# Four layers of cross attention and mixture of experts: routing the tokens per batch, the first batch inside the attention stream

## The chip, the cores and the metric

The kernel runs on one core of a Trainium2 chip. The metric is the device time of one execution in microseconds (us); before the change the median of three runs is 2267.55 (2266.69 to 2267.87). The engines are named as in the profile: PE (matrix multiply) and PEld (its weight loads), DVE (vector), ACT (scalar, with the function tables), POOL (GpSimd) and SP, whose queue issues most of the plain DMAs. Indirect DMAs (scatters and gathers by row number) are issued by POOL. All data is float32.

## What is computed

The state `x` has 2 batches of 512 tokens of width 256; the context has 2 batches of 1024 rows of width 256. Four layers follow each other, each a cross attention and a mixture of experts, both added to the state:

```python
x = x + L0_xattn(layernorm(x), ctx);  x = x + L0_ffn(layernorm(x))
x = x + L1_xattn(ctx, layernorm(x));  x = x + L1_ffn(layernorm(x))
x = x + L2_xattn(layernorm(x), ctx);  x = x + L2_ffn(layernorm(x))
x = x + L3_xattn(layernorm(x), ctx);  x = x + L3_ffn(layernorm(x))
```

- Attention: L0 has 16 heads of 64 with scores clipped to ±11; L1 8 heads of 64, whose keys are the context and the state itself; L2 16 heads of 16, causal; L3 16 heads of 16 with rotary positions.
- Mixture of experts, 8 experts each. A router gives every token 8 logits. L0: softmax, the best expert, its result times the probability (gated SiLU, inner width 1024). L1: the best expert on rows scaled by the sigmoid of the logit (inner width 512), plus a shared expert for all tokens. L2: the two best, weights by a softmax over their two logits (ReLU, 1024). L3: first `h = rmsnorm(x @ W_in.T)`; the router and the experts work on `h`; the two best (gated SiLU, 1024), each result RMS-normed, the weighted sum RMS-normed again and multiplied by `W_out`.

## The kernel before

The state stays in SBUF as `X`, 8 tiles of 128 tokens by 256; tiles 0 to 3 are batch 0 and 4 to 7 batch 1. The program is written with a framework whose scheduler places instructions on the engines by program order as priority and by its own model of when they are ready.

**Attention streams.** Work is cut into groups (a batch and some heads; batch 0 comes first) and slots of a group: L0 16 groups of 4 slots, L1 8 of 6, L2 8 of 8, L3 8 of 16. A slot issues scores of one group and products of an earlier one. What belongs to a whole group (query projection `pq`, division, output projection `po` at L1391, the addition to `X` at L1394) is put into a queue of Python generators, `Pieces` (L203), and the slots call a piece now and then between their own work; `share` (L218) spreads what is left over the places that are left, `drain` (L225) runs the rest, and `run_stream` (L230) drives L0 and L1. PE's order in a stream is fixed as written (`pe_in_order`, L188). L2 and L3 share `attend16` (L1202): a first pass (scores at L1298, their maxima on DVE at L1308), `with_maxima` (L1313), a second pass (scores L1355, exponentials on ACT L1356, and in L2 the causal mask on POOL, `affine_select` at L1360), products (L1331), and `divide` (L1365). When a batch's last group is divided, `add_out` (L1387) is queued as four pieces. Scores and pieces take their PSUM banks from one set of seven.

**Routing, after the attention of each layer, for all 8 tiles at once.** The layer norm of `X` (L72 to L98), transposes (L117) and their copies to SBUF, both on ACT (L122); the router logits, two matmuls in two passes per tile, that is 32 instructions (`router_logits`, L251); the choice of the best or the two best, small DVE operations on 128 x 64 (`first_of`, `two_best`, `two_gates`, L269 to L301); and `slots_of` (L332). That one counts, by 9 matmuls of triangular and all-ones matrices (L347 and L349, 18 instructions), how many tokens in front go to the same expert, and from it gives each token a slot: each expert owns one tile of 128 slots, and what doesn't fit goes to overflow tiles behind them. It also finds each overflow tile's expert (`wrow`) and the number of overflow tiles (`used`, read into registers).

`moe` (L404) then scatters the rows to their slots in DRAM (`xd`, L424): one indirect DMA for each tile and pick, so 8 in L0 and L1, 16 in L2 and L3. With two picks a token number rides in each row (column 257); DVE rewrites it for the second pick (L423), after the first pick's scatter of that tile has read the row. Behind them stands the filler, PE work that waits for no scatter: in L0 and L2 the next layer's keys and values (`ahead1`, `ahead16`, L545 to L617), in L1 the shared expert (L1467), in L3 none. Then the slot tiles run: weights of one expert (`w`, SP at L438, or POOL by row number for overflow tiles, L445), rows (`xs`, L452, which wait for all scatters), two transposes, the expert's matmuls (first `pa`, then `pg`, `y`), and the results to DRAM. `combine` (L530) or `add_results` (L519) gather them and add them to `X` with the gates.

L3's part (L1521 to L1589) has more steps before the router: norm and transposes, `ph` (`xT` times `W_in`), an ACT copy for each tile to `h` (L1556), the RMS norm of `h` (squares on ACT L1537, scaling on DVE L1546), transposes to `hnT`. Each FFN loads its router's weights (`rw`, in L0 with the bias `rb`, in L3 with `w_in`, `eb`, `inw`) when its pools are opened.

Of the kernel before, what the change touches and what calls it, by code (L numbers as in the profile page):

```python
# [17 lines left out]
P = 128  # L18
# [15 lines left out]
def tile_kernel(ctx: ExitStack, tc: tile.TileContext, d: dict, out: bass.AP):  # L34
# [50 lines left out]
    def norm_to(dst, src, norm, ts=None, split=False):  # L85


        t0, mv, r = norm
        if split:
            nb = small.tile([P, mv.shape[1]], F32, tag=f"nb{mv.shape[1]}", name="nb")  # L90
            nc.vector.scalar_tensor_tensor(nb, mv[:, :, 0], -1.0, r, ALU.mult, ALU.mult)
        for t in range(mv.shape[1]) if ts is None else ts:
            if split and t % 2:
                nc.scalar.activation(
                    dst[:, t0 + t, :], src[:, t0 + t, :], AF.Identity, bias=nb[:, t : t + 1], scale=r[:, t : t + 1]
                )
                continue
            nc.vector.tensor_scalar(  # L98
                dst[:, t0 + t, :], src[:, t0 + t, :], mv[:, t, 0:1], r[:, t : t + 1], ALU.subtract, ALU.mult
# [103 lines left out]
    class Pieces:  # L203
# [14 lines left out]
        def share(self, places):  # L218

            self.due += max(self.left, 0) / places  # L220
# [9 lines left out]
    def run_stream(n_groups, slots, lag, unit, prep, steps):  # L230
# [4 lines left out]
        while t < n_groups * slots + lag or pieces.queue:  # L235
# [4 lines left out]
            if u == slots - 1:  # L240
# [4 lines left out]
    def bc8(a):  # L245
        return a[:, :, None].to_broadcast([P, TT, E])

    def rt(name, shape=(TT, E)):
        return small.tile([P, *shape], F32, tag=f"rt_{name}", name=name, bufs=1)

    def router_logits(ps, srcT, w):  # L251
        pl = ps.tile([P, TT, E], F32, tag="mm", name="pl")
        for t in range(TT):
            mm2(pl[:, t, :], srcT, slice(t * P, (t + 1) * P), w, slice(0, E))
        lg = rt("lg")
        nc.vector.tensor_copy(lg, pl)
        return lg

    def maxed(src, name):
        m = rt(name, (TT,))  # L260
        nc.vector.tensor_reduce(m, src, AX.X, ALU.max)
        return m

    def summed(src, name):
        m = rt(name, (TT,))
        nc.vector.tensor_reduce(m, src, AX.X, ALU.add)
        return m

    def first_of(src, m, name):  # L269

        oh = rt(name)
        nc.vector.tensor_tensor(oh, src, bc8(m), ALU.is_equal)
        nc.vector.tensor_mul(oh, oh, rank)
        k = maxed(oh, "first_k")
        nc.vector.tensor_tensor(oh, oh, bc8(k), ALU.is_equal)
        return oh

    def two_best(src):
        oh1 = first_of(src, maxed(src, "m1"), "oh1")
        rest = rt("rest")  # L280
        nc.vector.scalar_tensor_tensor(rest, oh1, -3.0e38, src, ALU.mult, ALU.add)
        oh2 = first_of(rest, maxed(rest, "m2"), "oh2")
        return oh1, oh2

    def two_gates(lg, oh1, oh2):

        t = rt("pick")
        s = rt("sel", (2, TT))
        for i, oh in enumerate((oh1, oh2)):
            nc.vector.tensor_mul(t, oh, lg)  # L290
            nc.vector.tensor_reduce(s[:, i, :], t, AX.X, ALU.add)
        m = rt("selm", (TT,))
# [10 lines left out]

    def expert(ps, hp, srcT, w1, w2, F, act, glu, consume):

        FT = F // P
        for tb in range(2):
            cols = slice(tb * 512, (tb + 1) * 512)
            hT = hp.tile([P, FT, 512], F32, tag="hT", name="hT")
            for f in range(FT):  # L310
                pa = ps.tile([P, 512], F32, tag="a", name="pa")
                mm2(pa, w1, slice(f * P, (f + 1) * P), srcT, cols)
# [4 lines left out]
                mm2(pg, w1, slice(F + f * P, F + (f + 1) * P), srcT, cols)  # L317
# [14 lines left out]
    def slots_of(ps, picks, n_over):  # L332
# [3 lines left out]


        oh = rt("oh_all", (2 * TT + 1, E))
        nc.vector.memset(oh, 0.0)
        own = oh[:, TT : 2 * TT, :]  # L340
        if len(picks) == 1:
            nc.vector.tensor_copy(own, picks[0])
        else:
            nc.vector.tensor_add(own, picks[0], picks[1])

        pr = ps.tile([P, TT + 1, E], F32, tag="mm", name="pr")
        nc.tensor.matmul(pr, below, oh[:, TT:, :], start=True, stop=False)  # L347
        for k in range(1, TT + 1):
            nc.tensor.matmul(pr, ones, oh[:, TT - k : 2 * TT + 1 - k, :], start=False, stop=(k == TT))  # L349
        r = rt("rank_in", (TT + 1, E))  # L350
        nc.vector.tensor_copy(r, pr)
# [1407 lines left out]
```

## Time and profile before

| | us |
|---|---|
| median of three runs | 2267.55 (2266.69 to 2267.87) |
| the profiled execution | 2271.06 |
| its span | 2269.0 |
| L0 attention, FFN | 0 to 468.8, to 690.0 |
| L1 attention, FFN | to 1079.3, to 1235.0 |
| L2 attention, FFN | to 1400.7, to 1626.0 |
| L3 attention, FFN | to 1935.2, to 2269.0 |
| busy over the span: PE, DVE, ACT, POOL | 2087.4 (92%), 1085.2 (48%), 866.2 (38%), 438.6 (19%) |

The borders are the ends of the additions to `X` that close an attention, and the starts of the next one's first work; neighbouring stages overlap a little. The windows view gives the busy time of every engine in such a stretch, with the clock that was granted to PE (1.00 is full). The chain of waits goes back from the last instruction, at each step to what released it. Both speak of one execution, the profiled one.

### The profile page before, as it was taken

The page shows a single profiled execution, that of the slowest core. Times are in us where ns is not written, and L with a number is a line of the kernel's source. Part 1 is how long each engine was busy: PE and PEld are TensorE (multiplying, and loading weights), DVE is VectorE, ACT ScalarE, POOL GpSimd, SP SyncE. Part 2 cuts the span into 40 slices and gives each one's busy share as a digit, 9 for nine tenths or more (in the row PEclk, how much of TensorE's full clock was granted, in tenths as well). Part 3 has the DMA queues.
Part 4 walks back from the last instruction along what each step waited for, and adds up shares of the span by engine and source line. Part 5 has one row for each costly group of instructions (what it writes and reads, how often), then busy time and mean ns, then how long its engine had stood idle before and what let it go on. Part 6 is the DMA issues. An engine that isn't in the chain of part 4 may idle for free. (4 is left out here: it accounts for less than half of the span.)

```text
span 2269.0 us, 30730 instructions
## 1 busy us (share of the span) xinstructions
PE 2087.4 (92%) x11892; PEld 1267.6 (56%) x11892; DVE 1085.2 (48%) x2161; ACT 866.2 (38%) x1657; POOL 438.6 (19%) x420
## 2 busy tenths in 40 slices
PE   7999999999998999999898898899599999579996
PEld 3444444358984444555586344599333333479995
DVE  7766666741115656655313884110387773322223
ACT  4444444421115655555112333222135556223333
POOL 2222223210012111111101122312123310111110
PEclk9999999999999999999899999999789999689998
DMA  4222221277744101001454512687311101657771
GB/s 128 70 61 75 75 72 50 83 269 283 302 162 136 38 28 38 28 10 51 156 211 153 213 35 90 219 320 293 101 47 30 34 15 25 250 187 288 315 306 63
DMA packets 112328, 301.21 MB, mean 133 GB/s; under 512 B 23344, under 2 KB 76849, under 8 KB 103473
## 3 DMA queue, kind: packets, MB, share of 16 engines
q1 hardware_dynamic: 76624, 159.79, 21.0%
q0 software_dynamic: 9888, 104.49, 12.0%
q10 hardware_dynamic: 25664, 34.90, 4.3%
q8 instruction: 98, 1.61, 0.3%
q14 instruction: 54, 0.43, 0.1%
HBM read 243.42 MB, written 47.66 MB: 128 GB/s over the span
## 5 line engine op out<-in xcount | busy, mean ns | idle before, releaser
L1356 ACT ACTIVATE p<-s 128x512 f32<-128x512 f32 (+3 forms) x384 | 186.3, 546 | 176.2 <-PE s L1355 115.4
L132 PE MATMUL pa<-sT,w 128*128 128x128 f32 x1920 | 236.0, 277 | 10.7 <-DVE sT L462 3.7
L132 PEld LDWEIGHTS pa<-sT,w 128*128 128x128 f32 x1920 | 227.3, 193 | 19.3 <-ACT sq L1537 5.7
L480 PE MATMUL y<-w,hT 128*128 128x256 f32 x960 | 221.8, 383 | 12.4 <-DVE hT L477 6.3
L1298 PE MATMUL s<-kT,qT 32*128 32x512 f32 (+3 forms) x768 | 218.2, 613 | 10.0 <-DVE nm L1304 4.9
L480 PEld LDWEIGHTS y<-w,hT 128*128 128x128 f32 x960 | 178.5, 191 | 37.7 <-DVE hT L477 8.5
L1355 PE MATMUL s<-qA,kT 32*128 32x512 f32 (+3 forms) x768 | 196.1, 586 | 1.3 <-ACT p L1356 0.9
L1308 DVE TENSOR_REDUCE mx<-s 128x1 f32<-128x512 f32 x256 | 163.5, 686 | 56.1 <-PE s L1298 35.4
L477 DVE TENSOR_TENSOR hT<-act,pg 128x512 f32<-128x512 f32 x82 | 56.0, 688 | 233.5 <-PE pg L132 204.6
L1043 ACT ACTIVATE p<-s,nm 128x512 f32<-128x512 f32 x192 | 129.6, 687 | 84.0 <-DVE nm L1040 84.0
L132 PE MATMUL pg<-sT,w 128*128 128x128 f32 x1312 | 160.0, 275 | 1.3 <-ACT sv L575 1.3
L878 ACT ACTIVATE p<-s 128x1024 f32<-128x1024 f32 x128 | 124.3, 1023 | 89.7 <-PE s L873 89.7
L879 DVE TENSOR_SCALAR p<-p 128x1024 f32<-128x1024 f32 x128 | 108.9, 859 | 95.2 <-ACT p L878 95.2
L132 PEld LDWEIGHTS pg<-sT,w 128*128 128x128 f32 x1312 | 153.1, 192 | 1.4 <-ACT sv L575 1.4
L1040 DVE TENSOR_REDUCE nm<-s 128x2 f32<-128x1024 f32 x96 | 113.3, 1221 | 83.5 <-PE s L1036 83.5
L149 POOL TENSOR_TENSOR kT<-kT,turned 128x512 f32<-128x512 f32 x62 | 100.8, 1631 | 215.2 <-DVE turned L147 208.4
L884 DVE TENSOR_TENSOR acc<-acc,p 128x1024 f32<-128x1024 f32 x96 | 131.6, 1371 | 2.8
L804 PE MATMUL o<-p,v 128*64 128x512 f32 x512 | 125.7, 609 | 3.6 <-DVE p L879 3.6
L873 PE MATMUL s<-qT,kT 64*128 64x512 f32 x512 | 127.2, 615 | 0.0
L1298 PEld LDWEIGHTS s<-kT,qT 32*128 32x128 f32 x768 | 77.1, 191 | 66.7 <-issue 28.0
L1057 PEld LDWEIGHTS pt<-ident,p 128*128 128x128 f32 x768 | 86.3, 141 | 49.2 <-issue 24.5
L1331 PE MATMUL o<-p,v 128*32 128x256 f32 (+3 forms) x1280 | 106.2, 403 | 6.7 <-POOL p L1360 6.4
(282 smaller groups left out, 2955.3 us busy)
## 6 DMA issues: line engine op xcount, KB each, us to landing
w<-in_L_experts_dram SPq DMA_DIRECT2D x8, 3200.0 KB
w<-in_L_experts_dram SPq DMA_DIRECT2D x8, 3072.0 KB
w<-in_L_experts_dram SPq DMA_DIRECT2D x8, 2048.0 KB
w<-in_L_experts_dram SPq DMA_DIRECT2D x8, 1536.0 KB
kd<-sk ACTq DMA_DIRECT2D x40, 256.0 KB
kT<-kd SPq DMA_DIRECT2D x16, 512.0 KB
turned<-kT SPq DMA_DIRECT2D x60, 128.0 KB
v<-vd SPq DMA_DIRECT2D x12, 512.0 KB
```

The source lines that it names most:

```text
L132: nc.tensor.matmul(ps_ap, lhsT[:, dc, lcols], rhs[:, dc, rcols], start=(dc == 0), stop=(dc == 1))
L480: nc.tensor.matmul(y, hT[:, f, :], w2[:, f, :], start=(f == 0), stop=(f == FT - 1))
L804: nc.tensor.matmul(G[n]["o"][64 * j : 64 * j + 64, :], V[g, b][:, kt, pr * P + 64 * j : pr * P + 64 * j + 64], p[:, j, :], start=(kt == 0) ...
L873: nc.tensor.matmul(s1[:, j, :], G[n]["kT"][r, kt * P : (kt + 1) * P], G[n]["qT"][r, :], start=True, stop=True)
L878: G[n]["exp"] = nc.scalar.activation(p, s1, AF.Exp, scale=0.125).ins
L884: nc.vector.tensor_add(G[n]["acc"], G[n]["acc"], p)
L1040: nc.vector.tensor_reduce(nm[:, qt, :, c], s1, AX.X, ALU.max, negate=True)
L1043: nc.scalar.activation(p[:, j, :], s1[:, j, :], AF.Exp, bias=nm[:, qt, j, c : c + 1], accum_out=l[:, qt, j, c : c + 1],)
L1298: nc.tensor.matmul(s1[:, :w], qT[r, qt * P : (qt + 1) * P], kT[r, c * 512 : c * 512 + w], start=True, stop=True)
L1308: nc.vector.tensor_reduce(mx[:, qt, j, c : c + 1], s1, AX.X, ALU.max)
L1355: nc.tensor.matmul(s2[:, qs], kT[r, kt * P : (kt + 1) * P], qA[r, qs], start=True, stop=True)
L1356: nc.scalar.activation(p[:, j, qs], s2[:, qs], AF.Exp, scale=0.25)
```

## The change

The functions that routed all tiles at once are replaced by a class `Dispatch`, made once per layer. Its generators do the steps for one batch of four tiles (`norm`, `turned`, `logits`, `to_slots`, the scatters included), and `last` does what needs both batches (`wrow`, `used`). `dispatch0` to `dispatch3` string them together for a layer. Batch 0 is queued as pieces into the attention's stream, when the first batch's part of `X` is final; batch 1 runs after the attention as before. `yield` marks the end of a piece; `gap` puts empty pieces between steps.

What changes with it:

- For batch 1, `to_slots` adds the counts of batch 0, and gives a second step (`far`) to ranks beyond the overflow tiles that batch 0 opened. The number of expert tiles that run is the same; the order of the overflow tiles can differ.
- The prefix matmuls are 5 per batch (10 instructions) in place of 9 for all.
- Of the two copies of a transposed batch one is on ACT, one on DVE (`copy_alt`).
- The router's weights are loaded before or at the start of the attention, into a pool that stays until the end of the layer (`apart`).
- L1's sigmoid becomes exp, +1 and a reciprocal.
- L3's `ph` is two banks of two tiles with one copy each; the first batch's scratch tiles in L3 come from four buffers of the pool `L3y`, which also take the gathered results of L2.
- At the end of a stream `run_stream` no longer drains; it goes on with slots until the queue is empty, and there `share` calls pieces as long as the queue holds any.

The core of the diff:

```diff
         def share(self, places):
 
-            self.due += max(self.left, 0) / places
+            self.due += max(self.left, places == 1 and len(self.queue)) / places
...
             unit(t, pieces)
-            if u == slots - 1:
+            if u == slots - 1 and n + 1 < n_groups:
                 pieces.drain()
...
+        def norm(self, b, pool, bank, tags=("xn", "xT")):
+
+            S = self.S[b]
+            S["rows"] = pool.tile([P, 4, self.width], F32, tag=tags[0], name="xn")
+            norm_to(S["rows"][:, :, 0:D], X, norm_of(X, 4 * b, 4), d0=0)
+            yield
+            yield from self.wait(b)
+            S["xT"] = pool.tile([P, 2, 512], F32, tag=tags[1], name="xT")
+            yield from self.turned(S["xT"], S["rows"], bank)
...
+        def to_slots(self, b, picks, bank):
...
+            pr = bank("pr")[:, 0 : 5 * E].rearrange("p (t e) -> p t e", e=E)
+            nc.tensor.matmul(pr, below, oh[:, 4:9, :], start=True, stop=False)
+            for k in range(1, 5):
+                nc.tensor.matmul(pr, ones, oh[:, 4 - k : 9 - k, :], start=False, stop=(k == 4))
...
+            yield
+            more = rt(b, "more", (E, 7))
...
+            rows, named = S["rows"], self.width > D
+            for i, si in enumerate(S["slots"]):
+                if named and i == 0:
+                    nc.vector.tensor_copy(rows[:, :, D], c_tok[:, 4 * b : 4 * b + 4])
+                for t in range(4):
+                    if i == 1:
+                        c = 4 * b + t
+                        nc.vector.tensor_scalar(rows[:, t, D:], c_tok[:, c : c + 1], float(NT), None, ALU.add)
+
+                    x = nc.gpsimd.indirect_dma_start(
+                        out=xds[self.L][0], out_offset=bass.IndirectOffsetOnAxis(ap=si[:, t : t + 1], axis=0),
+                        in_=rows[:, t, :], in_offset=None,
+                    ).ins
...
+            if t == 4 * (len(groups) - 1):
+                pieces.add(dispatch0(0, dp, banks(ps)), 10)
...
+            if (n, w) == (5, 0):
+                pieces.add(dispatch1(0, dp, lambda name: ps.tile([P, 512], F32, tag="mm", name=name, bufs=3)), 12)
...
                         if groups[m - 1][1] == 3:
                             pieces.add(add_out(groups[m - 1][0]), 4)
+                            pieces.add(dispatch(bank), 9 + 6 * rotary)
...
+        all_of(dispatch2(1, fp, banks(ps)))
+        disp.last()
...
+    def dispatch3(b, pool, bank, tags, hpool):
+
+        S = disp.S[b]
+        yield from disp.norm(b, pool, bank, tags[:2])
+        h = S["rows"] = hpool.tile([P, 4, D + 1], F32, tag="h", name="h")
+        for k in range(2):
+            ph = bank("ph").rearrange("p (t f) -> p t f", t=2)
+            for i in range(2):
+                c = (2 * k + i) * P
+                mm2(ph[:, i, :], S["xT"], slice(c, c + P), w_in, slice(0, D))
+            nc.scalar.copy(h[:, 2 * k : 2 * k + 2, 0:D], ph)
+            yield
+        rms(pool, tags[2], h, inw, 0, 4)
+        yield
+        yield from disp.wait(b)
+        hT = pool.tile([P, 2, 512], F32, tag=tags[3], name="hT")
+        yield from disp.turned(hT, h, bank)
+        yield from disp.logits(b, hT, rw, bank)
...
+        yield from disp.to_slots(b, picks, bank)
+
+    attend16(
+        "L3", params, 8, False, True, False, lambda bank: dispatch3(0, ay, bank, ["yg"] * 4, dp), first, late
+    )
```

## The prediction

> **What bounds the kernel now.** I read the windows by stage first (layer by layer, attention and FFN apart), then the chain of waits in the stages that the change touches, then the timeline at the borders. The profiled execution took 2271.06 us (span 2269.0, 2.1 around it), 3.5 over the median of three, 2267.55. I work in its clock and take the difference off the median. Columns of the windows: stretch, length, PE, PEld, DVE, ACT, POOL busy, granted clock, DMA share, GB/s. Here are L3's attention, L3's FFN and eight microseconds of the end of L0's attention.
>
> ```profile
> 452.00:456.00 4.00, 1.78 (x8) 0.20 (x4) 3.96 (x4) 0.00 (x0) 0.47 (x1) 1.00 0.00 0
> 456.00:460.00 4.00, 3.93 (x10) 1.00 (x10) 1.49 (x3) 0.00 (x0) 0.00 (x0) 0.57 0.00 0
> ...
> 1626.00:1935.20 309.20, 301.11 (x2210) 111.15 (x2210) 207.68 (x380) 151.75 (x277) 65.71 (x51) 0.95 0.12 35
> 1935.20:2269.00 333.80, 271.77 (x1884) 252.22 (x1884) 87.93 (x305) 113.00 (x207) 48.46 (x50) 0.89 0.61 239
> ```
>
> L3's attention has PE busy 97% and DVE 67%: work added to it is paid for. Its FFN has PE busy 81%, and the chain shows where the rest is: no filler covers the way from the last addition to X (ends 1935.22) to the first expert matmul (pa, 1999.19).
>
> ```profile
> 1937.08 2.19 PE pt L117 x8
> ...
> 1955.29 7.01 PE pl L132 x32
> ...
> 1966.86 3.43 PE pr L349 x16
> ...
> 1973.98 1.01 POOL xd L424
> ...
> 1993.04 2.56 DMA xd<-h,si
> ...
> 1995.79 2.08 DMA xs<-xd
> ...
> 1999.19 3.55 PE pa L132 x16
> ```
>
> That gap is 64.0 us; 19.1 of it, 1973.98 to 1993.04, is POOL issuing 16 scatters, the logits run at half speed (.219 us each; L0's 32 took 3.63 at clock 1.00, .114 each). In L0, L1 and L2 a filler (next layer's keys, or the shared expert) keeps PE busy meanwhile, so only L3's gap is bare.
>
> **L3, the gap.** Each per-token step halves. Scatters 16 to 8, at a pitch of 19.06/15 = 1.27: −10.2. Logits 32 to 16: −3.5. Copies and squares on ACT (1942.27 to 1949.24, .87 a tile), four tiles less: −3.5. Transposes of xn (4.06): −2.0. Scaling and transposing h (2.87 + 1.77): −2.3. Prefix matmuls 18 to 10 (4.1): −1.8. Choice (narrower rows): −.3. Six more slot operations in the chain at .22: +1.3. Sum −22.3, taken as −22; the new gap is 42. The 14 small operations of `last` (14 × .2 = 3) lie behind eight scatters (10.1); uncovered they cost 3. The first weights, issued 1934.83 and in flight until 1965.3, put a floor of some 30 under it: not reached.
>
> **L3, the stream.** PE takes on 16 transposes (1.04 per 8: 2.1), 16 ph matmuls (3.62), 16 logits (1.8), 10 prefix (1.25): 8.7. What does PE work cost there? The chain holds one pq a group:
>
> ```profile
> 1796.72 1.91 PE pq L132 x4
> ...
> 1813.68 1.92 PE po L1391 x8
> ...
> 1835.82 1.91 PE pq L132 x4
> ```
>
> Groups lie 31.65 apart (1733.43 to 1765.08, to 1796.72) without po, and 39.10 with four po of 1.92: 7.45 longer for 7.68 of work, .97 for one. So +8.5. ACT gets the square roots among the exponentials: two pairs of table loads at 1.28, 5.1 on an engine that is half free; I take +1.5 of 0 to 5. DVE gets some 13 us (about 45 small operations at .2, four applies at .33, four scalings at .41, copies at .6) into its free third of two groups (23). And a wait comes with it: between the picks DVE rewrites the token number (L423) of each tile, which waits for that tile's first scatter. Before, these stood 1.2 apart after a first 2.3, so four hold DVE for about 6, and behind it queue the maxima (mx, 1.3 a slot) that free PSUM banks for PE's next scores. Seven banks and the scheduler, which may put maxima between, hide most: +1 of 0 to 6. Stream +11 (5 to 18); L3 −11 (−17 to −4).
>
> One page of the Trainium skill speaks against this. The row first: at 2078.75 a table load takes 1.28 and the square root follows at 2080.05, so 1.30 a switch. "ScalarE: Activation LUTs", section "What ACT_TABLE_LOAD costs", adds a drain of about 1.38 to the load's 1.28, 2.66 a switch; by it L3's four would be an estimated 10.6 instead of 5.1, and with the same share falling on PE's path (1.5 of 5.1) the stream would cost 3.1 for them and the whole sum come to −7. No drain is seen in that row, so the row decides.
>
> **L1.** Its filler starts late because the router weights are late and PE's clock is cold:
>
> ```profile
> 1088.87 6.97 PE L132 MATMUL pl<-rw,xT 128*128 128x8 f32 x32 [4.62 <-DMA rw<-in_L_ffn_router_wT_dram]
> 1095.69 2.06 PE L132 MATMUL pa<-xT,w 128*128 128x512 f32 x2
> ```
>
> With the weights loaded before the attention, 4.62 of waiting and half of the logits (3.5) go, and half of the prefix (1.8), which ran inside the filler. What is late next is the shared expert's w1, issued 1083.7 to 1084.6 and by rw's 5.6 us an estimated 1090 to 1091.6 on the chip; so −7 (−5 to −9). The filler ended 1143.6 and the experts began 1144.99, so it passes on. The stream gets 8 transposes, 16 logits, 10 prefix: 4.1 on a PE that is 96% busy, and 1 for tables: +5. L1 −2 (−6 to +1).
>
> **L0.** The dispatch falls into the last slots, about 436 to 460, where DVE sets the pace (3.96 of 4 busy in the first line above, PE 1.78; the clock of .57 in the second is PE coming back from that idleness). A unit there is 3.79 us: PE 1.99 for scores and 1.94 for products, DVE twice .69 and 1.23, 3.84. The dispatch adds some 8 us of DVE work (applies, one copy, some 30 small operations; the statistics of batch 0 already ran there before); of the 22 us from 436 to 458 DVE had 3.3 free: +5, and 1 for the tables. Behind, PE's filler ended 508.2 and the rows landed about 507, together; PE loses 3.8 of work (8 transposes 1.04, 16 logits 1.8, 8 prefix 1.0), the scatters shift by more: −4. L0 +2 (−4 to +7).
>
> **L2.** The queue that matters is POOL's. In the causal stream POOL masks every probability tile, and PE waits for it:
>
> ```profile
> 1380.18 1.06 PE L1331 MATMUL o<-p,v 128*32 128x512 f32 x8 [1.65 <-POOL p L1360]
> 1380.54 0.41 POOL L1360 TENSOR_SCALAR_AFFINE_SELECT p<-p 128x256 f32<-128x256 f32 x1 [0.42 <-ACT p L1356]
> ```
>
> The dispatch is queued behind the first batch's four products (the last po at 1360.45) as nine pieces and more, one in each slot or every second one, of some 1.9 us. By that count the eight scatters (8 × 1.27 = 10.1 of POOL) come out near 1375 to 1385, among the last group's nine masks (1376.6 to 1387.8). Price 0 to 10.1; PE's wait of 5.3 in 1376 to 1400 is the nearest row, I take 6, a little above it, since scatters that start between two masks delay only the next. DVE's hold at the token numbers falls into the same time and is not counted twice. PE work of 4.1 costs .53 of itself (pitch 15.25, then 18.33 with three po, 5.76), +2. Behind: PE loses 4.1 before the filler's end and some 2 of stalls: −6. L2 +2 (−6 to +9).
>
> The early loads of router weights on SP's queue are small and go ahead of loads with 40 us and more to spare (L0's issue 459.75, needed 505); uncovered, the rw row's 4.6 is the price of one. No other SP instruction moves; the expert tiles are as many as before.
>
> **Sum:** −11 −2 +2 +2 = −9: 2271.06 becomes 2262, and off the median 2258.5.
>
> **Rivals.** *The streams hide it.* L3's stream pays only half (+5), as in L2 where .53 was paid; masks and scatters interleave. −17 −4 −1 +0 = −22: 2245.5. Against it stands L3's .97. *It cancels.* L3's stream pays its upper part, +16 (tables 3, the DVE hold 4.5), L1 0, L0 and L2 +3 each: −6 +0 +3 +3 = 0: 2267.5. *The scatters block the in-order queues,* on the slower side: in both two-pick streams eight scatters in one piece, 10.1, stand ahead of what the attention waits for, L2's masks and L3's rotations and maxima, at full price. L3 −22 +10 +10 = −2, L2 +2 +10 −6 = +6, L0 with DVE full +5, L1 −2: +7, 2274.5. It decides once the attention's own instruction is queued behind the first scatter rather than between two. For it speaks that DVE's L147 in L2 ran only at 1433.75, straight behind eight such waits; against it, POOL works only 21% of L3's attention. *The gap doesn't shrink,* because weights and not rows end it: excluded by the 30 us floor, short of a slower transfer.
>
> **Chances.** Forecast .42 (2251 to 2265), hidden .20, cancels .16, blocked .22. Below 2263.0 (0.2% is 4.5 us, about what can be told from no change) lie the hidden case and .36 of the forecast: .56. Within: .16 and .06: .22. Slower: .22. The range, 2243 to 2277, reaches into both outer cases and leaves out .07 below and .10 above; the forecast's own is 2251 to 2265.
>
> **What would show it.** L3: last addition to X until first pa near 42, the group with the dispatch some 11 longer. L2: masks behind scatters, attention's end later by about 8. L1: no wait for rw, filler 4 to 6 earlier after the attention. L0: attention's end later by about 6. Table loads for square roots inside all streams. The forecast falls if L3's gap stays over 50 or its stream grows by under 6 or over 16.

## The result, and the profile after

The changed kernel takes 2300.77 us (median of four runs, 2299.67 to 2311.03), the kernel before 2267.71 on the same chip (2266.69 to 2270.84): a ratio of 1.0154 [1.0123, 1.0184], 1.5% slower, where 2258.5 was forecast. The profiled execution after took 2300.8; its span is 2299.1, before 2269.0, so 30.1 longer. By the ends of the additions to `X` (for L3's FFN by the start of the last one):

| stage | before | after | difference | forecast |
|---|---|---|---|---|
| L0 attention, FFN | 468.8, 214.4 | 477.6, 213.6 | +8.8, −0.8 | +6, −4 |
| L1 attention, FFN | 396.0, 152.6 | 406.0, 144.2 | +10.0, −8.4 | +5, −7 |
| L2 attention, FFN | 168.9, 226.0 | 189.8, 234.9 | +20.9, +8.9 | +8, −6 |
| L3 attention, FFN | 308.5, 329.8 | 318.1, 310.6 | +9.6, −19.2 | +11, −22 |

L3, where the gain was expected, came out as forecast (−9.6 against −11). L2 lost 29.8 where 2 was forecast, and L0 and L1 lost 9.6 where 0 was. Here are the windows of after, with the columns of the prediction: the end of L0's stream, then L3's attention and FFN.

```profile
452.00:456.00 4.00, 4.00 (x28) 2.22 (x24) 3.88 (x5) 1.59 (x2) 1.70 (x1) 1.00 0.17 59
456.00:460.00 4.00, 4.00 (x18) 1.30 (x18) 3.86 (x9) 2.16 (x3) 0.00 (x0) 1.00 0.00 0
460.00:464.00 4.00, 0.48 (x4) 0.48 (x3) 3.29 (x11) 0.00 (x0) 0.00 (x0) 0.78 0.00 0
464.00:468.00 4.00, 4.00 (x15) 2.50 (x17) 1.99 (x15) 0.00 (x0) 0.00 (x0) 0.50 0.01 4
...
1666.10:1984.20 318.10, 308.12 (x2268) 116.93 (x2268) 218.53 (x440) 161.00 (x296) 73.47 (x59) 0.97 0.18 58
1984.20:2299.00 314.80, 261.50 (x1828) 242.65 (x1828) 85.66 (x304) 106.02 (x187) 40.69 (x42) 0.91 0.59 228
```

In L0 the stream now runs some 9 us longer; at 460 PE stands still (0.48 of 4) while DVE makes the choice, and the next four microseconds run at half clock. In L3's attention PE works 7.0 more (301.11 before) and DVE 11. That this stage met its forecast is in part luck: its time at half clock fell from 31 us to 18 (the table below), at its start, ahead of the dispatch. The chain of waits over L3's gap:

```profile
1998.52 3.60 PE pl L133 x16
...
2006.19 6.24 issue
2012.43 0.27 POOL xd L424
...
2021.32 2.43 DMA xd<-h,si
...
2023.95 1.96 DMA xs<-xd
...
2027.33 3.75 PE pa L133 x16
```

16 logits and 8 scatters instead of 32 and 16: from the last addition (1984.18) to the first `pa` it is 43.2 us, 64.0 before. In L1 nothing waits for the router weights any more; the timeline of PE:

```profile
1102.63 3.16 PE L133 MATMUL pl<-rw,xT 128*128 128x8 f32 x14 [0.15 <-DVE xT L184]
```

What is new stands in L2. SP's timeline there has the four loads of the first expert weights apart, where they were one group before. Behind it stand SP's longest wait ahead of them (line, for whom, us in total, times, longest) and the group of before:

```profile
1427.10 0.35 SPq L510 DMA_DIRECT2D w<-in_L_experts_dram  x1
...
1440.22 0.33 SPq L510 DMA_DIRECT2D w<-in_L_experts_dram  x1
...
1470.86 0.44 SPq L510 DMA_DIRECT2D w<-in_L_experts_dram  x1
...
1480.58 0.43 SPq L510 DMA_DIRECT2D w<-in_L_experts_dram  x1
```

```profile
SPq L510 <- DVE oT L1497: 24.7, 1, 24.7
```

```profile
1265.36 2.30 SPq L438 DMA_DIRECT2D w<-in_L_experts_dram  x4
```

Before (third fence), all four went out at 1265, early in L2's attention. After, the first waits until the attention is at its end, for the division (L1497) that reads the last `rec`; the others queue behind it, and 3 of the 4 fall into the filler, whose own small writes of keys and values then wait: ACT's waits for them (`sk` and `sv` behind DMA `kd` and `vd`) are 41.4 us in L2's FFN instead of 20.3. The cause is an address. Tiles for four token tiles instead of eight make L2's FFN pool smaller, what is laid behind it slides down, and the first weight buffer (bytes 150720 to 167104 of a partition) now overlaps the attention's last `rec` (149088 to 151136) by 416 bytes. These addresses come from the layout of the program and not from the trace; e1 below tries them.

And there is the queue of POOL. First PE's longest wait towards the end of L2's stream after (1370 to 1432; columns as in the line on SP), then the one of before (1340 to 1401), then POOL's timeline after, and what ACT and PE do there:

```profile
PE o L1445 <- POOL p L1474: 12.5, 6, 5.1
```

```profile
PE o L1331 <- POOL p L1360: 6.4, 5, 1.6
```

```profile
1407.12 1.04 POOL L424 DMA_INDIRECT xd<-xn,si  x1 [0.98 <-DVE slot_pick L409]
...
1411.01 0.96 POOL L424 DMA_INDIRECT xd<-xn,si  x1 [0.30 <-issue]
1411.98 0.77 POOL L1474 TENSOR_SCALAR_AFFINE_SELECT p<-p 128x256 f32<-128x256 f32 x2
...
1417.93 0.96 POOL L424 DMA_INDIRECT xd<-xn,si  x1 [0.30 <-issue]
1418.91 0.41 POOL L1474 TENSOR_SCALAR_AFFINE_SELECT p<-p 128x256 f32<-128x256 f32 x1
```

```profile
1407.48 1.00 ACT L1470 ACTIVATE p<-s 128x256 f32<-128x256 f32 x4 [1.87 <-PE s L1469]
...
1412.45 1.08 PE L1445 MATMUL o<-p,v 128*32 128x256 f32 x8 [5.00 <-POOL p L1474]
```

The scatters come at 1407 to 1419, not at 1375 to 1385, and the last masks stand behind them: those of 1411.98, whose exponentials ACT had done by 1408.48, behind all four scatters of the first pick.

### The profile page after: what moved, and what is told of

The parts are those of the page before. It is cut to its first block, busy times and chain, and to the rows that moved or that the text cites. A ratio compares the mean times of both kernels' runs of the same rounds, so it can differ in the third digit from the quotient of the medians.

```text
span 2299.1 us, 30980 instructions
## 1 busy us (share of the span) xinstructions
PE 2108.5 (92%) x11900; PEld 1275.6 (55%) x11900; DVE 1117.2 (49%) x2374; ACT 873.6 (38%) x1662; POOL 439.4 (19%) x420
## 4 chain that ended last, share of the span: by engine, by line
PE 50%; DMA 7%; DVE 6%; ACT 3%; issue 3%; POOL 2%; SPq 0%; ACTq 0%; POOLq 0%; DVEq 0%
PE pa L133 6%; PE y L552 6%; PE s L1412 5%; PE s L1469 4%; PE o L1445 4%; PE pg L133 4%; PE s L1148 3%; PE pt L1169 3%; PE o L1178 3%; PE pq L133 2%; PE pk L133 2%; DMA yd<-yo,ti 2%; ACT p L1155 1%; DMA xs<-xd 1%; DVE nm L1152 1%
## 5 line engine op out<-in xcount | busy, mean ns | idle before, releaser
L1469 PE MATMUL s<-qA,kT 32*128 32x512 f32 (+3 forms) x768 | 202.2, 599 | 2.8 <-DVE qA L1433 1.2
L150 POOL TENSOR_TENSOR kT<-kT,turned 128x512 f32<-128x512 f32 x62 | 100.4, 1625 | 221.9 <-DVE turned L148 203.3
```

Source lines behind the costliest of these rows:

```text
L1469: nc.tensor.matmul(s2[:, qs], kT[r, kt * P : (kt + 1) * P], qA[r, qs], start=True, stop=True)
```

## The experiments

Two theories. *Space and queues:* L2's weights wait for an address, its masks for scatters, and each can be taken away alone. *The clock:* a short stall of PE costs more than its length, because the clock stays at half behind it; then what a stage loses is read from its time at half clock. The table has the stages of each profiled execution; in brackets the time at half clock, from the records of the granted clock (about 2 × (1 − PEclk) × the length of a window). The last column is the median, over a kernel's runs, of the time multiplied by the mean granted clock. A stage is read from one execution, so small differences say little: with the code of before, L2's attention lies between 168.1 and 172.8 in eleven kernels, L1's between 396.1 and 398.6 in eight.

| run | median us | ratio, 95% | L0 and L1 | L2 attention | L2 FFN | L3 attention | L3 FFN | us × clock |
|---|---|---|---|---|---|---|---|---|
| before | 2267.7 to 2271.6 | | 1231.8 | 168.9 (17) | 226.0 | 308.5 (31) | 329.8 | 2184 |
| after | 2300.8 | 1.012–1.018 | 1241.4 | 189.8 (48) | 234.9 | 318.1 (18) | 310.6 | 2202 |
| e1 | 2306.5 | 1.015–1.019 | 1237.5 | 189.8 (48) | 220.9 | 341.9 (66) | 310.6 | 2191 |
| e2 | 2299.5 | 1.011–1.015 | 1237.2 | 189.8 (48) | 220.2 | 342.4 (73) | 310.9 | 2188 |
| e3 | 2301.8 | 1.012–1.016 | 1238.0 | 178.4 (38) | 228.0 | 342.7 (74) | 310.6 | 2191 |
| e4 | 2288.4 | 1.006–1.010 | 1233.1 | 168.3 (17) | 226.2 | 344.5 (75) | 311.3 | 2185 |
| e5 | 2291.5 | 1.007–1.012 | 1233.9 | 172.8 (27) | 223.5 | 326.3 (64) | 331.1 | 2185 |
| e6 | 2288.4 | 1.006–1.012 | 1231.6 | 169.8 (21) | 228.2 | 342.6 (70) | 309.0 | 2183 |
| e7 | 2278.3 | 1.002–1.006 | 1233.0 | 172.4 (31) | 224.5 | 335.9 (32) | 311.1 | 2200 |
| e8 | 2303.3 | 1.011–1.019 | 1233.0 | 196.8 (65) | 214.9 | 342.4 (66) | 310.5 | 2189 |
| e9 | 2271.5 | 1.000–1.002 | 1229.5 | 170.6 (24) | 226.6 | 323.3 (39) | 313.9 | 2184 |
| e10 | 2275.1 | 1.000–1.003 | 1231.8 | 172.8 (27) | 224.7 | 332.0 (42) | 308.0 | 2187 |
| e11 | 2277.3 | 1.002–1.005 | 1239.2 | 182.2 (41) | 225.4 | 320.7 (25) | 306.3 | 2189 |
| e12 | 2292.9 | 1.008–1.013 | 1235.6 | 202.6 (44) | 217.2 | 322.1 (26) | 307.8 | 2206 |
| e13 | 2283.3 | 1.004–1.007 | 1223.5 | 168.3 (17) | 224.3 | 343.1 (70) | 307.7 | 2185 |
| e14 | 2275.6 | 0.999–1.003 | 1227.3 | 171.4 (27) | 224.3 | 336.1 (60) | 308.9 | 2184 |
| e15 | 2297.6 | 1.010–1.013 | 1232.9 | 182.7 (41) | 225.8 | 342.6 (72) | 307.8 | 2185 |
| e16 | 2300.9 | 1.011–1.016 | 1231.0 | 182.8 (17) | 224.9 | 346.3 (77) | 310.0 | 2205 |
| e17 | 2269.6 | 0.999–1.002 | 1229.2 | 168.1 (17) | 224.8 | 323.3 (39) | 317.0 | 2186 |
| e18 | 2260.7 | 0.996–1.000 | 1224.3 | 168.3 (17) | 221.9 | 307.5 (28) | 329.4 | 2181 |

**e1_pad_l2: the address.** The change with a tile of 512 bytes that nobody uses ahead of the others in L2's FFN pool:

```diff
+        fp.tile([P, 128], F32, tag="pad", name="pad")
         all_of(dispatch2(1, fp, banks(ps)))
```

> The changed kernel with one unused tile of 512 bytes per partition ahead of the others in the pool of L2's FFN; nothing else. Theory of space: in the change the first expert weight buffer of L2 lies 416 bytes over the last buffer of the attention's rec (150720 to 167104 against 149088 to 151136), so its load waits for the end of the attention and the three behind it on SP's queue too; with the tile it lies clear, the four loads are issued early in the attention again (as at 1265 in the kernel before), L2's FFN gets 9 to 15 us shorter, and the time is 2286 to 2292. Theory of queues: L2's FFN is longer because the dispatch of batch 1 leaves PE cold and the writes of the filler wait for each other; the tile changes nothing, 2299 to 2302.

L2's FFN fell by 14.0, from 234.9 to 220.9, and SP issued the four weights in one group:

```profile
1271.31 1.88 SPq L510 DMA_DIRECT2D w<-in_L_experts_dram  x4
```

The space theory holds for this term: 220.9 is 5.1 below before, where −6 was forecast. But the kernel didn't get faster. L3's attention, in which nothing was edited, took 341.9 instead of 318.1.

**e2_pads.** e1, and L1's normalised state put where no tile of L0's FFN lay:

```diff
-        to_T(ps, xT, normed(cp, True, "oT"), TT, g_l, b_l, "s")
+        to_T(ps, xT, normed(dp, True, "xn8"), TT, g_l, b_l, "s")
```

> As the kernel with the 512 bytes, and L1's normalised state in a place of its own on the far side of SBUF. Theory of space: in the change this tile lies over L0's transposed context cT (88064 to 104448 both begin there), so its 8 scalings wait 9.1 us for the last key matmul; freed of that, L1's attention begins some 4 to 5 us earlier, 2282 to 2288. If that wait was hidden by the keys' way through DRAM anyway, no difference to the kernel with the 512 bytes.

L1's attention went from 404.3 (e1) to 403.0: that overlap is worth 1.3 at most. L3 again 342.4.

**e3_l2_after.** e1 with L2's first batch dispatched behind the attention:

```diff
-    hold = attend16(..., lambda bank: dispatch2(0, dp, bank))
+    hold = attend16(..., None)
...
+        all_of(dispatch2(0, dp, banks(ps)))
         all_of(dispatch2(1, fp, banks(ps)))
```

> As the kernel with the 512 bytes, but in L2 the first batch is dispatched after the attention too, ahead of the second. Theory of the in-order queues: L2's stream is 21 us longer because of the pieces in it (table loads on ACT, matmuls that wait for DVE on PE, scatters among the masks on POOL); without them it is as long as before (169 us from the end of L1's FFN to the last addition to X), and the filler hides nearly all of the second dispatch: 16 to 21 less than with the 512 bytes alone, 2267 to 2274. Theory of space: the stream is longer because of where the tiles lie; then the stream stays near 185 us, and the time near 2286.

The attention fell by 11.4 to 178.4, and the FFN grew by 7.1. 9.5 of the 20.9 stay: the framework's scheduler still put the first batch's norm (statistics, root, applies) into the stream, at 1369 to 1376, since its input was ready there. Its time at half clock is 20.4 above before, and half of that is 10.2, an estimate of what it costs. Neither expectation was met.

**e4_only_l3.** L0 to L2 with the code of before (all eight tiles behind the attention), L3 as in the change. For L2, and L0 and L1 likewise:

```diff
-        all_of(dispatch2(1, fp, banks(ps)))
-        disp.last()
+        layernorm(xn[:, :, 0:D], X, TT, False)
+        to_T(ps, xT, xn, TT)
+        lg = router_logits(ps, xT, rw)
+        oh1, oh2 = two_best8(lg)
+        disp.send(ps, xn, [oh1, oh2], two_gates8(lg, oh1, oh2))
```

> L0, L1 and L2 dispatch as in the kernel before (all eight tiles after the attention, router weights loaded there), L3 as in the change. If the layers add up as the two traces say (L0 +8.0, L1 +1.6, L2 +29.8, L3 -9.3), this is 9.3 below the kernel before: 2256 to 2261. If L3's part was gained only because of something in the other layers (the clock, where its tiles lie), it is within 4 of the kernel before, 2264 to 2271.

Missed by 30. L3's FFN gained its 18.5, but its attention took 344.5. The windows of e4, from the start of L3's attention on:

```profile
1627.60:1919.20 291.60, 284.32 (x2066) 107.37 (x2066) 211.80 (x420) 145.13 (x268) 69.33 (x55) 0.94 0.12 36
1919.20:1924.60 5.40, 2.00 (x14) 0.46 (x12) 0.41 (x2) 0.22 (x2) 2.88 (x3) 1.00 0.32 100
1924.60:1962.10 37.50, 36.87 (x156) 9.04 (x156) 0.00 (x0) 13.88 (x27) 1.26 (x1) 0.50 0.30 106
```

And ACT's timeline, then PE's, at that place:

```profile
1917.94 1.26 ACT L1595 ACTIVATE p<-s 128x512 f32<-128x512 f32 x2
1924.38 2.06 ACT L1595 ACTIVATE p<-s 128x512 f32<-128x512 f32 x4 [5.18 <-remote]
```

```profile
1920.07 1.13 PE L1594 MATMUL s<-qA,kT 32*128 32x512 f32 x4
1925.03 1.56 PE L1570 MATMUL o<-p,v 128*32 128x256 f32 x8 [3.83 <-ACT p L1595]
```

ACT stands still for 5.18 us with its scores ready; PE, in its fixed order, waits 3.83 for it; and then the clock is at 0.50 for 37.5 us, although PE is busy 36.87 of them. Half of 37.5 is 18.8 of the 26.4 by which e4's L3 attention exceeds that of after. The rest needn't be the standstill: at the start of the stage e4 has some 37 us at half clock where after has 18, an estimated 9.7 more. The same standstill (3.9 to 5.4 us, at the same instruction of ACT) is in e1, e2, e3, e6, e7, e8, e13, e15 and e16; it is not in after, e11 and e12.

**e5_hold: the clock alone.** The kernel before, and right behind the second-last group's `ou` copy in L3:

```diff
+                    if rotary and m == NG - 1 and k == 2:
+                        nc.scalar.copy(xT[:, 0, 0:512], G[m - 1]["ou"])
+                        for _ in range(2):
+                            nc.scalar.copy(xT, xT)
```

> The kernel before, with nothing of the change: in L3's attention, right after the second-last group's ou copy, ACT makes three copies that nobody needs (0.6, 2.4 and 2.4 us by the 0.59 that a 512-wide copy takes), so 5.4 us on an engine that is half free. Clock theory (a stall of a few us drops TensorE's clock to half, and the rest of the last group, made of matmuls on 32-row tiles, stays there): L3's attention grows from 308.5 to 325 to 335, with half clock for 30 to 45 us from the stall on, the kernel 2283 to 2293. Rival (the stall costs its own length only): 308.5 + 2 to 6 = 311 to 315, the kernel 2269 to 2273.

326.3, and 2291.5 for the kernel: the clock theory's numbers. The three copies took 4.4 us (0.62, 1.89 and 1.90), PE waited 2.39 for the exponentials behind them, and the stage got 17.8 longer. The window of e5 behind them:

```profile
1909.20:1950.20 41.00, 40.26 (x162) 11.36 (x157) 2.13 (x5) 14.50 (x26) 1.26 (x1) 0.50 0.09 27
```

So no part of the change is needed for such a loss, only a stall at this place.

**e6_late_scatters.** e4 with the first batch's scatters called behind the attention:

```diff
+        disp.scatter(0, 0)
+        second = dispatch3(1, fp, ...)
+        next(second)
+        next(second)
+        disp.scatter(0, 1)
+        all_of(second)
```

> L0 to L2 as before and L3's first batch in the stream, as in e4, but its eight scatters are issued behind the attention (four ahead of the second batch's norm, four behind its first transposes). If the scatters in the stream set off ACT's standstill of 5.2 us and with it the half clock: L3's attention 315 to 320 instead of 344.5, its FFN 311 to 314, the kernel 2258 to 2264. If they don't: attention 340 to 345, the kernel 2285 to 2290.

The edit didn't do what it says: the scheduler issued the scatters at 1913 to 1922, inside the stream, as soon as their inputs were ready. It is e4 a second time, with e4's time. e9 mends it.

**e7_warm.** e4 with matmuls that nobody reads:

```diff
+                    if rotary and m == NG - 1 and k == 3:
+                        hot = bank("hot")
+                        for _ in range(16):
+                            nc.tensor.matmul(hot, perm16, cos[:, 0:N], start=True, stop=True)
```

> e4 with 16 matmuls of 128x128 by 512 columns that nobody reads put into PE's order two slots behind the place of ACT's standstill. Clock theory (full 128-row matmuls bring the clock back, 32-row ones don't): the half-clock stretch falls from 37.5 us to 15 to 20, which saves 9 to 11 and costs some 5 of matmuls: L3's attention 336 to 341 instead of 344.5, s matmuls behind them at 0.59 instead of 1.2. Rival (the clock stays low whatever PE does, or the slot is long for another reason): 344.5 + 4 to 7 = 349 to 352 and 37 us of half clock or more.

335.9, just under the 336 to 341, and 10 us off the kernel; but not by bringing the clock back. They ran from 1920.4 to 1934.4 (14 us, not some 5), filled PE while ACT stood still for 5.2, and the clock never fell. That PE's idleness in the standstill starts the half clock is supported; whether 128-row matmuls end it isn't tested. They aren't needed for it: in e4 the clock came back at 1962.19, ahead of the first 128 x 128 matmul (1962.64), when PE had no scores left but only products:

```profile
1958.73 3.17 PE L1570 MATMUL o<-p,v 128*32 128x256 f32 x24
```

**e8_no_root.** e1, the first batch's roots left out (`bare` is set for batch 0 alone; the rows are scaled wrongly):

```diff
+        if bare:
+            nc.vector.tensor_scalar(r, src, scale, eps, ALU.mult, ALU.add)
+            nc.vector.reciprocal(r, r)
+            return r
...
-        r = recip_sqrt(mv[:, :, 1], n, 1.0, LN_EPS)
+        r = recip_sqrt(mv[:, :, 1], n, 1.0, LN_EPS, bare)
```

> e1 (the change, with the 512 bytes in L2's FFN pool) without the square roots of the first batch's norms (four layers) and of L3's inner norm: the reciprocal is taken of the variance itself, so the rows are scaled wrongly and the output differs; four to five pairs of table loads go from the streams. If the table loads among the exponentials are what starves PE in the causal stream (e3 kept them there and kept 9.5 us of L2's loss): L2's attention 178 to 182 instead of 189.8, L0's 474 to 475 instead of 476.6, L3's one table pair less in its tail. If POOL's queue is: L2's attention 188 to 190. L3's half-clock stretch isn't expected to go by this: total 2290 to 2298 by the first, 2304 to 2308 by the second.

The table loads are not it: L2's attention took 196.8, 7 more than with them, and its half clock 65 us instead of 48. Of the attentions only L1's got shorter (404.3 to 400.6). In L2 the clock fell at 1369.3, with PE busy nearly throughout. The windows of e8 around it:

```profile
1362.00:1366.00 4.00, 4.00 (x35) 2.29 (x33) 3.07 (x13) 0.63 (x3) 1.82 (x3) 1.00 0.01 4
1366.00:1369.30 3.30, 3.06 (x19) 1.62 (x16) 3.23 (x13) 3.01 (x7) 0.96 (x2) 0.99 0.02 4
1369.30:1372.70 3.40, 3.40 (x15) 0.66 (x15) 2.08 (x6) 0.24 (x1) 0.41 (x1) 0.50 0.02 1
```

In the middle one PE has almost nothing but scores on 32 rows. The busy share of the profile alone doesn't tell the clock.

**e9_late_scatters.** e6, with a true dependence on the last addition:

```diff
+            nc.vector.scalar_tensor_tensor(
+                self.S[0]["rows"][:, :, D], X[:, 7, 0:4], 0.0, c_tok[:, 0:4], ALU.mult, ALU.add
+            )
+            self.scatter(0, 0)
```

> e6 again, since there the scatters were still issued inside the stream, at 1913 to 1922. Now the token numbers that the scatters carry are written with a reading of the last tile of X, so none can start before the attention's last addition. If the scatters in the stream set off ACT's standstill of 5 us: no standstill, no long half-clock stretch, L3's attention 314 to 320 instead of 344.5, its FFN 311 to 316, the kernel 2258 to 2266. If they don't: 340 to 345 again, the kernel 2285 to 2290.

No standstill and no long half clock in the tail; attention 323.3, over the 314 to 320, FFN 313.9. The kernel, at 2271.5, is as fast as before and no faster: the stream's +14.8 eats the 15.9 that the FFN gains. Some of it is clock again: 6.8 us of its half clock are at 1877 and 1894, among the dispatch's pieces, where before had none.

**e10_earlier.** e4 with

```diff
-    disp = Dispatch("L3", 2, 1)
+    disp = Dispatch("L3", 2, 0)
```

> e4 with the pauses taken out of L3's dispatch (gap 0 instead of 1), so that its pieces and the eight scatters come some four to six slots (6 to 10 us) earlier in the last group but one. If the standstill is the meeting of the scatters with the last exchange of inverses (four small transfers and the eight scatters between 1917 and 1922 in e4): the scatters are through before it, no standstill, L3's attention 314 to 320, the kernel 2258 to 2266. If the standstill hangs on the place in ACT's own program: it stays right behind the ou copy, attention 340 to 345, the kernel 2285 to 2290.

The standstill is gone from its place, but ACT waits twice some 4 us near 1902 and 1914, where the pieces now come thick, and the attention takes 332.0. Half of the expectation: its first clause held, its time didn't.

**e11_L2_late: POOL's queue.** e1, L2's scatters held behind the attention with the dependence of e9:

```diff
+        disp.first_late()
+        second = dispatch2(1, fp, banks(ps))
...
+        disp.scatter(0, 1)
```

> e1 with L2's first eight scatters held behind the attention by the same dependence; everything else of L2's dispatch stays in the stream. POOL-queue theory (the prediction's: scatters among the masks): L2's attention 180 to 183 instead of 189.8. Clock theory (the stall that drops the clock comes earlier, at 1373 to 1394, from the table loads and the late exponentials): 187 to 190, half clock in L2's attention still near 48 us. In its FFN the filler's rotations queue behind the scatters on POOL, up to +5.

182.2, within the POOL theory's 180 to 183 (182.7 in e15, with the same L2): the scatters cost 7.6 there, 3.4 of it by the estimate from half clock (41 us for 48). The FFN, where they now stand, grew by 4.5. PE's wait for the masks in this kernel's stream:

```profile
PE o L1458 <- POOL p L1487: 4.5, 5, 1.6
```

8.0 less than in after. L3 had no standstill here (320.7), with the code that had one in e1.

**e12_L2_warm.** e1 and, in L2's stream,

```diff
+                    if L == "L2" and t == 66:
+                        hot = bank("hot")
+                        for _ in range(16):
+                            nc.tensor.matmul(hot, perm16, xT[:, 0, 0:N], start=True, stop=True)
```

> e1 with 16 matmuls of 128x128 by 512 columns that nobody reads put into PE's order in L2's attention, two slots into the tail of the last group (about 1394 in the profile after). Clock theory: the half-clock time of L2's attention falls from 47.8 us to 15 to 25, which is worth 11 to 16, and the matmuls cost 3.5 (full clock) to 7: 178 to 186 instead of 189.8. Rival (the time goes to POOL's queue and the clock only follows it): 193 to 197, with half clock still over 40 us.

202.6, the wrong side: they took PE 14 us (1386.3 to 1400.3), and the clock fell behind them all the same, at 1405.15. The first scatter came only at 1413.47; in after the clock fell at 1394.09 and the first scatter came at 1407.12. So the half clock of L2 doesn't begin with the scatters. My price for the matmuls was too low here too.

**e13_L3_and_rw and e14_later.** e13 is e4 with L1's router weights loaded ahead of the attention; e14 is e13 with gap 2.

```diff
         to_T(ps, xT, normed(cp, True, "oT"), TT, g_l, b_l, "s")
+        rw = load_rows(dp, d["L1_ffn_router_wT"], "rw")
...
-        rw = load_rows(fp, d["L1_ffn_router_wT"], "rw")
```

> L0 to L2 as before, L3's first batch in the stream as in e4, and L1's router weights loaded ahead of its attention (L1 otherwise as before). L1's filler no longer waits 4.62 for them: L1's FFN 147 to 149 instead of 152. L3 as in e4 if its standstill returns (attention 340 to 345, the kernel 2279 to 2285), or as in the change without it (318 to 323 and 307 to 311, the kernel 2255 to 2262, which would beat both kernels).

> e13 with longer pauses in L3's dispatch (gap 2 instead of 1), so that the scatters come some six slots later, behind the last exchange of inverses. If the standstill needs scatters beside the exchange: none, attention 316 to 324, FFN 308 to 314, the kernel 2255 to 2264. If it needs only the place in the code: attention 340 to 345, the kernel 2279 to 2285.

L1's FFN fell to 146.8 and 149.0, as expected. e13's standstill returned (343.1); its profiled execution (2272.85) is the fastest of its five. In e14 ACT waited 3.0 at 1920 (for PE's scores, by the profile) and 1.7 more at 1924, the half clock lasted 27 us there, and the attention took 336.1: between the two theories. Its eleven runs lie between 2254 and 2285 at mean clocks of 0.968 and 0.956; the same program with more or less half clock.

**e15_L0_L1_behind.** e11 and, for L0 (L1 likewise),

```diff
-            if t == 4 * (len(groups) - 1):
-                pieces.add(dispatch0(0, dp, banks(ps)), 10)
...
+        all_of(dispatch0(0, dp, banks(ps)))
```

> e11 with the first batch of L0 and of L1 dispatched behind the attention, as L2's was in e3; tiles, pools and L1's early router weights stay as in the change. If the pieces in the streams are what lengthens them: L0's attention 467 to 470 instead of 478.8, L1's 396 to 400 instead of 405.9, and their FFNs 1 to 4 longer each, the kernel 2262 to 2270. If it is the layout or the clock: 475 and 403 or more.

L0's attention fell from 478.8 to 470.4 and L1's from 405.9 to 398.7: the pieces in the streams cost 8.4 and 7.2. The FFNs grew by 3.2 and 6.1 (1 to 4 was expected), so dispatching the first batch early loses 5.2 in L0; in L1 it loses 1.1, which is within the spread. The total (2297.6) missed because the standstill was back in L3.

**e16_e4_L2_shifted.** e4 with the four lines of e12.

> e4 with the 16 matmuls of e12 in L2's attention; L3's program is e4's to the instruction. If ACT's standstill hangs on what ran before (time, clock), it can go: L3's attention 316 to 324 as in e12, the kernel 2262 to 2275. If it belongs to e4's program: attention 340 to 345, the kernel 2288 to 2298.

346.3: the standstill stayed. Another timing ahead of it isn't enough to remove it.

**e17_late_and_rw and e18_rw_alone.** e17 is e9 with the edit of e13; e18 is the kernel before with that edit alone.

> e9 (L3's first batch in the stream, its eight scatters behind the attention) with L1's router weights loaded early. Summed from the parts: L1's FFN 147 to 149 instead of 152, L3's attention 314 to 323, its FFN 310 to 314, the kernel 2258 to 2268: faster than before by 0.2 to 0.5%. If the clock at the start of L3's attention or in its tail goes the other way: 2270 to 2276, no gain.

> The kernel before with one edit: L1's router weights are loaded ahead of its attention. The wait of 4.62 in L1's FFN goes: 147 to 149 instead of 152.6, all else as before, the kernel 2264 to 2268 beside its 2268 to 2272. If the time that it saves is lost again to the clock or to the shared expert's weights, which are late next: within 1 of before.

e17 is as fast as before (ratio 0.9989 to 1.0021), above its 2258 to 2268. e18's L1 FFN took 146.2 instead of 152.6, and its median is 8 us under before's, but its interval, 0.9964 to 1.0003, still holds 1: likely a little faster, not shown. No version was shown to beat the kernel before.

## Why the prediction was wrong

**What held.** L3's gap: 43.2 for the forecast 42, by the steps named (logits 3.60 for 16, scatters 8.9 from the start of the first to that of the last, 19.06 before). L3's stream: +9.6 for +11; PE's added work was 7.0 and DVE's 11, for 8.7 and 13. But the total of this term was met by luck: with 31 us at half clock as before and not 18, it would have been an estimated +16, and in the nine kernels that had the standstill, without dense matmuls in L3, it was +33 to +38, past the prediction's own limit of 16. L1's filler: −8.4 for −7. L2's FFN without its address: −5.1 for −6 (e1).

**What failed first: "No other SP instruction moves; the expert tiles are as many as before."** They are as many, but the loads of their first weights do move: the first went out at 1427 instead of 1265. The step counted instructions and left out that a tile's address decides what its load waits for. 14.0 of the 30.1 (e1).

**L2's stream, +8 forecast, +20.9 measured.** Three terms, by e3 and e11: 9.5 while only the norm is in the stream, 3.8 for the other pieces of PE and DVE (2 was forecast), 7.6 for the scatters (6 was taken, from a bound of 0 to 10.1). The scatters' price came out nearly right, but they were placed 30 us too early, and its reason, that scatters between two masks delay only the next, didn't hold: the masks stood behind four (1411.98). What was missing is the 9.5, and e3's half clock (20.4 us more than before, half of it 10.2) accounts for it. It was no term of the sum at all. What sets that half clock off stays open: without the table loads it was longer (e8), and it begins ahead of the scatters (after, e12).

**L0, +6 and −4 forecast, +8.8 and −0.8 measured.** e15 gives the stream's part, 8.4. At 460 to 464 PE's fixed order lets the attention's last products wait behind the counting matmuls, which wait 3.5 for DVE's choice; the sum had DVE's 8 us but not this order. The FFN's −0.8 lies in the spread: 210.3 to 213.9 in the six kernels with this code in L0, that is −4.1 to −0.5. **L1, +5 forecast, +10.0 measured:** 7.2 are the pieces (e15), up to 1.3 the overlap of its first tile with L0's context (e2); the rest is open.

**The rivals.** *The scatters block the in-order queues* is what L2 shows, at 7.6 of its 10.1; in L3's stream of after they cost nothing that can be seen, but without them e9's was 21.2 shorter than e4's. At 2274.5 it gave the right sign and under a quarter of the loss. Neither it nor the forecast had a term for the clock: every price was a length of work or of a wait at the clock of the row it came from. That is the common fault; by (1 − clock) × span, at most 99.2 us were lost to the clock after and 85.5 before, by this estimate 13.7 of the 30.1. Multiplied by the mean granted clock, before and all the kernels from e1 to e18 but three come to 2181 to 2191, while their times run from 2261 to 2306; the three (e7, e12, e16) have dense matmuls added, and after has L2's late weights. That doesn't make the dispatch free in work; the product adds up gains and costs. Taking half of its time at half clock off each stage (a rough estimate, since half clock costs nothing where PE is idle), the four streams of e1 are 36.0 longer than before (L0 7.8, L1 6.6, L2 5.7, L3 15.9) where 30 was forecast, and the four FFNs 29.5 shorter (3.2, 7.4, 8.2, 10.7) where 39 was. (In L3's FFN the other 8.5 of the 19.2 are half clock that went with the gap.) So the streams paid somewhat more than was forecast for their work. Of the 36.0 by which e1's whole span exceeds that of before this balance leaves 6.5; the other 29 are clock.

**Left open.** Why ACT stands still for 4 to 5 us at one instruction in ten of the thirteen kernels that have the scatters at that place in L3's stream. The records show its input ready, no semaphore in between, and no packet of instructions in that time. With the scatters behind the stream (e9, e17) it is absent, but it is also absent with them in three kernels.

## What to carry to other kernels

Price work that is moved into a busy stream by the clock too: at a place where only narrow matmuls follow, 4.4 us of copies on a half-free engine cost 17.8 (e5). When a change makes a pool smaller, compare the addresses of the buffers that are prefetched next with the tiles still in use: 416 bytes cost 14 us, and 512 unused bytes gave them back (e1). And read each stage by itself: L3's FFN was 13 to 24 us shorter in every kernel that had the halved gap, and the gain was lost elsewhere.

## What the runs showed of the hardware

**Half clock under a busy PE.** All stretches at half clock are multiples of 3.41 us (37.5 is eleven), but for the one that the end of the run cuts. PE's own instructions agree with the record: eight products take 1.08 in it and 0.64 ahead of it (e4). The Trainium skill, "TensorE: Matmul & The Clock Gate", section "Part 1: The HAM clock gate (the "warmup" mystery)", describes this free-running window of 3413 ns and says that one busy window brings full clock back. The first part agrees. The second doesn't for scores on 32 rows in turn with products on 32 columns: in e4 the clock stayed at 0.50 for eleven windows with PE busy 98%, and came back with a window that held next to nothing but products. In e8 it fell behind a window that was 93% busy. The measurement decides: for such matmuls the busy time of the profile doesn't tell the clock.

**A standstill without a releaser.** 5.18 us of ACT in e4 that the profile puts down to "remote", and 3.95 to 5.37 at the same instruction in nine more kernels; nothing recorded explains it.

**Scatters on POOL.** Eight issues of 0.96 at a pitch of 1.27. A mask of 0.41 that comes among them waits for all that stand ahead of it on POOL, not for one only: in after PE waited 5.00 and 5.12 us for the two masks behind them.
